# Two banded layers on one core: transposes by halves of rows, and a new order of TensorE's work in a step

## The chip, the cores and the metric

The kernel runs on one core of a Trainium2 chip. The core has a matrix engine (TensorE, PE in the profile, its weight loads shown apart as PEld), a vector engine (DVE), an activation engine (ScalarE, ACT), a general engine (GpSimd, POOL) and a queue that issues nearly all transfers (SyncE, SP). Each engine takes its own instructions in program order and waits on semaphores for the others. TensorE writes to PSUM alone, eight banks of 512 fp32 values on each of 128 partitions; DVE and ScalarE carry the results to SBUF. The metric is the time on the device in microseconds.

## The reference

Two layers of the same form run one after the other on `x` (512 x 512 x 64, fp32): `x = x + layer(_gn(x))`, where `_gn` normalises by groups of two channels over the whole picture. A layer is

```python
xn = _ln(x, norm_scale, norm_bias)                       # over the 64 channels
left = (xn @ Wl + bl) * mask * sigmoid(xn @ Wlg + blg)   # 64 -> 128
right = (xn @ Wr + br) * mask * sigmoid(xn @ Wrg + brg)
out_gate = sigmoid(xn @ Wog + bog)
out = _banded_ingoing(left, right, 4)   # out[i,j,h] = sum over d in -4..4 of left[i+d,i,h] * right[i+d,j,h]
out = _ln(out, out_norm_scale, out_norm_bias) * out_gate
return out @ Wo + bo
```

The kernel does the sum over the band as a matrix product for each channel `h`: a banded 64 x 64 matrix of `left` values times the rows of `right`.

## The kernel before

**Tiling.** Blocks of `S = 64` rows are worked one after the other. A tile has 128 partitions: 64 rows at columns `j` (lower half) and the same 64 rows at columns `256 + j` (upper half). A *unit* is `JU = 8` columns in each half; 16 units (`NU`) make a *chunk* of 128 columns in each half, and there are 18 chunks a layer. The two halves never mix: projections, gates and band products take partitions 0 to 63 and 64 to 127 in separate matmuls, each with its own 64 rows of the matrix engine.

**One step.** The loop in `layer` (L731 on) emits one *step* `t` for every unit. It works on several units at different stages: it loads units ahead, normalises unit `t + 2` (`inner_norm`, POOL), transposes unit `t + 1` so that channels lie on partitions (`transposed`, L430), projects unit `t` to `right` values (`right`, L459, in two halves of four columns), and finishes the output of a unit of 30 steps ago (`outs[t]`). For that it reads the unit's transposed input back from DRAM (`recall`, L590, tile `zg` with two buffers), computes the gates (`gates`, L594), transposes the normalised band sums `on` (`turned`, L613), multiplies them by the gates on DVE into `ZH`, and a step later multiplies by `Wo` (`end`, L643) and adds the residual rows `XR`, which `fetch` (L632) loaded. In layer 1 `sums` adds up statistics for the group norm of layer 2. At the end of a step come zero, one or two `mix` calls (L511), the band products; ten steps of a chunk have 16 of them, six have none. A mix writes its results over `RO`, the buffer of `right` values.

**Order.** All engines get this order as it is written (`keep_in_program_order`, L362, which is why nearly every row of the profile has that line). On TensorE a step is: gates (two matmuls of 64 rows by 128 columns, every fp32 matmul as two instructions), projection (eight matmuls, the same shape), `left` in five early steps, four transposes of `z` and eight of `on` (128 x 128, one instruction each), `end` (16 matmuls of 128 rows by 64 columns), `sums`, and the mixes (64 by 64). ScalarE evacuates gates, sigmoids of the projection, `zT`, then computes the eight `on` of the next step (`norm`, one buffer), then copies mixes. DVE does statistics (`sto` of RO, `sti` of z), the products into RO, ZH, the residual add, and part of the copies. POOL does the affine (`ga`, `gb`), `inner_norm`, the bias onto `XR` (`biased`) and, in every fourth step, the reciprocal root behind `solve`, whose first operation DVE issues (`rs`).

**Queues and buffers.** SyncE issues in a step: loads of z, `zg` for step `t + 2`, `XR` for step `t + 1`, the matrices A (`take_left`), the store of `zT`, the stores of finished rows. An issue that must wait for its buffer holds all behind it. PSUM: pairs of banks (`two_banks`, two of them) for projections and mixes; single banks (`one_bank`, three in layer 1, four in layer 2) for gates, transposes and `end`.

Of the kernel before, what the change touches and what calls it, by code (L numbers as in the profile page):

```python
# [8 lines left out]
F32 = mybir.dt.float32  # L9
I32 = mybir.dt.int32  # L10
AF = mybir.ActivationFunctionType
ALU = mybir.AluOpType
# [4 lines left out]
P = 128  # L17
WIN = 4
NEAR = 2 * WIN + 1
S = 64  # L20
JC = 128
JW = 16
JU = 8
JQ = 4
NU = JC // JU
# [54 lines left out]
def tile_two_banded_layers(  # L80
# [8 lines left out]
    H = layers[0]["Wl"].shape[1]  # L89
    x, out = x[0], out[0]  # L90
# [22 lines left out]
    ident = const.tile([P, P], F32, name="ident")  # L113
# [14 lines left out]
    def one_bank():  # L128
        return ps.tile([P, 512], F32, tag="ps", name="bank")

    def two_banks():
        return ps2.tile([P, 1024], F32, tag="ps2", name="banks")
# [220 lines left out]
    w = views(pack)  # L353
# [66 lines left out]
    def inner_stats(u: Unit, st: bass.AP, k: int):  # L420

        en.vector.bn_stats(st[:, k, :], u.z[:, 2 * k : 2 * k + 2, :].rearrange("p t c -> p c t"))

    def inner_norm(u: Unit):
        z = u.z.rearrange("p (k t) c -> p k t c", t=2)
        m = u.mean.unsqueeze(3).broadcast_to([P, JU // 2, 2, D])
        en.gpsimd.tensor_tensor(z, z, m, ALU.subtract)
        en.gpsimd.tensor_tensor(u.z, u.z, last(u.rs, D), ALU.mult)

    def transposed(u: Unit):  # L430

        u.t = ztp.tile([P, JU // 2, P], F32, tag="zT", name="zT")
        pt = one_bank()
        for k in range(JU // 2):
            en.tensor.transpose(
                pt[:, k * P : (k + 1) * P],
                u.z[:, 2 * k : 2 * k + 2, :].rearrange("p j c -> p (j c)"), ident,
            )
        en.scalar.activation(u.t.rearrange("c k p -> c (k p)"), pt, AF.Identity, bias=1.0)
        if u.near is None:  # L440
            en.sync.dma_start(later[u.at], u.t)

    def place(k: int, e: int) -> int:

        return k // 2 * 4 + 2 * e + k % 2
# [13 lines left out]
    def right(u: Unit, q: int, w: dict):  # L459
        pr = projected(u, q, w["right"]).rearrange("p e k h -> p (e k) h")  # L460
        sg = wk.tile([P, JQ, H], F32, tag="sg", name="sg", bufs=2)
        en.scalar.activation(sg, pr[:, :, H:], AF.Sigmoid)
        en.vector.tensor_tensor(
            RO[:, :, u.c + q : u.c + q + JQ, :],
            pr[:, :, :H].rearrange("p j (h t) -> p h j t", t=2),
            sg.rearrange("p j (h t) -> p h j t", t=2), ALU.mult,
        )
# [31 lines left out]
    def take_left(n: int, h: int) -> bass.AP:  # L499


        A = lp.tile([P, S, HA], F32, tag="A", name="A")
        at = n * size + h * slab + WIN * HA
        for e in range(2):
            en.sync.dma_start(
                A[e * S : (e + 1) * S].rearrange("p i h -> p (i h)"),
                strided(left_of, at, ((S + 2 * WIN) * HA, S), (1, S * HA)),
            )
        return A
# [80 lines left out]
    def recall(o: Out):  # L590
        o.t = ztg.tile([P, JU // 2, P], F32, tag="zg", name="zg")
        en.sync.dma_start(o.t, later[o.at])

    def gates(o: Out, w: dict):  # L594
        b = o.blk
        o.g = []
        pgs = [
            one_bank()[:, : 2 * JQ * b.m].rearrange("h (k p) -> h k p", p=b.m) for e in range(2)
        ]
        for e, pg in enumerate(pgs):  # L600
            part = slice(e * D, (e + 1) * D)
            en.tensor.matmul(
                pg, lhsT=w["gate"][part],
                rhs=o.t[part].rearrange("c k (e p) -> c (k e) p", e=2)[:, :, b.lo : b.hi],
                start=True, stop=True,
            )
        for pg in pgs:
            g = gp.tile([H, 2 * JQ * (S - WIN)], F32, tag="gate", name="gate")
            g = g[:, : 2 * JQ * b.m].rearrange("h (k p) -> h k p", p=b.m)
            en.scalar.activation(g, pg, AF.Sigmoid)  # L610
            o.g.append(g)

    def turned(o: Out, w: dict):  # L613

        b = o.blk
        for e in range(2):
            pt = one_bank()
            for k in range(JQ):
                en.tensor.transpose(
                    pt[:, k * P : (k + 1) * P], o.on[:, place(k, e), :], ident  # L620
                )
            zh = ZH[(2 * o.n + e) % len(ZH)]
            en.vector.scalar_tensor_tensor(
                zh[:, :, : b.m], pt.rearrange("h (k p) -> h k p", p=S)[:, :, b.lo : b.hi], w["ob"], o.g[e],
                ALU.add, ALU.mult,
            )

    def rows_of(v: bass.AP, o: Out, e: int):
# [14 lines left out]
    def end(dst: bass.AP, o: Out, w: dict):  # L643
        m = o.blk.m
        po = one_bank().rearrange("i (j c) -> i j c", c=D)
        for k in range(JQ):
            for e in range(2):
                for n in range(2):

                    en.tensor.matmul(  # L650
                        po[n * S : (n + 1) * S, 2 * k + e, :],
                        lhsT=ZH[(2 * o.n + e) % len(ZH)][:, 2 * k + n, :], rhs=w["Wo"],
                        start=True, stop=True,
                    )
        f = o.xr[: S + m, :, 1 : 1 + 2 * D]
        en.vector.tensor_tensor(
            f, po[: S + m].rearrange("i (k t) c -> i k (t c)", t=2), f, ALU.add
        )
        for e in range(2):
            en.sync.dma_start(rows_of(dst, o, e), o.xr[e * S : e * S + m, :, 1 : 1 + 2 * D])  # L660
# [13 lines left out]
    def layer(src: bass.AP, dst: bass.AP, w: dict, stats: bool, then=None):  # L674
# [32 lines left out]
        def inputs(t: int) -> list:  # L707
            return [d[t] for d in (units, lefts) if t in d]
# [22 lines left out]
        for t in range(min(loads), last_t + 3):  # L731
            if then and t == max(units) + 2:
                then()
            for u in loads.get(t, []):
                if u not in early:
                    load(src, u)
            if t + 2 in outs:
                recall(outs[t + 2])
            if t + 1 in outs:
                fetch(src, outs[t + 1], w, t + 1)  # L740
            for c, h in slabs.get(t, []):
                A[c, h] = take_left(c // per, h)

            for o in looks.get(t, []):
                if sto is None:
# [7 lines left out]
                affine(u, en.vector if u.at < NU + 4 else en.gpsimd)  # L753
            if t % 4 == 3 and t > NU:
                then_affine = affines.pop(t + 1, [])
            if t in outs:
                gates(outs[t], w)

            todo = []
            for at, u in inners.get(t, []):  # L760
# [7 lines left out]
                us.append(u)  # L768
            for v in todo[: len(todo) // 2]:
                inner_stats(*v)  # L770
            if t in units:
                for q in range(0, JU, JQ):
                    right(units[t], q, w)
            if t in lefts:
                for q in range(0, min(JU, NEAR * JQ - lefts[t].near), JQ):
                    left(lefts[t], q, w)
            for u in inputs(t + 2):
                inner_norm(u)
            for u in inputs(t + 1):
                transposed(u)  # L780
            if t in outs:
                turned(outs[t], w)
                biased(outs[t], w, stats)
            for v in todo[len(todo) // 2 :]:
                inner_stats(*v)
# [104 lines left out]
    lp = ctx.enter_context(tc.tile_pool(name="lp", bufs=NA))  # L890
    wk = ctx.enter_context(tc.tile_pool(name="wk", bufs=3))
    onp = ctx.enter_context(tc.tile_pool(name="onp", bufs=1))
    gp = ctx.enter_context(tc.tile_pool(name="gp", bufs=2))

    next(one, None)
    nc.sync.dma_start(pack, spare)
# [35 lines left out]
```

## Time and profile before

| | |
|---|---|
| median of 3 runs | 5074.44 us (5072.06 to 5078.64) |
| profiled execution, its own time | 5074.14 us |
| span from its first to its last instruction | 5072.3 us |
| TensorE busy, matmul / weight load | 4496.1 / 3714.8 us |
| DVE / ScalarE / GpSimd busy | 3732.8 / 3793.8 / 3826.9 us |
| transposes of `on`, 128 x 128 | 4608, mean 274 ns |
| transposes of `z`, 128 x 128 | 2344, mean 290 ns |
| products for the end, `bank<-pack,ZH` | 18432, mean 225 ns |
| granted TensorE clock, mean | 0.978 |

The profile is one execution. Rows name an operation by output and inputs: `bank<-ident,on` is the transpose of `on` into a single bank. Matmuls overlap and their ends are modelled, so a stage's length is read from the start of its first instruction to the start of the next stage's. A bracket in a timeline row is the idle time ahead of it and what ended that. Layer 1 works from about 306 to 2550 us, layer 2 from about 2709 us to the end.

### The profile page before, as it was taken

How to read it: one execution, taken by the hardware profiler on the slowest of the kernel's cores; microseconds unless marked ns; L12 is line 12 of the kernel's file. 1: busy time of each engine (PE TensorE's matmuls, PEld its weight loads, DVE VectorE, ACT ScalarE, POOL GpSimd, SP SyncE). 2: the span in 40 equal slices, each digit the busy share in tenths (PEclk: the TensorE clock that was granted, in tenths of full speed). 3: DMA queues.
4: the chain of work that ended last, by engine and by line, in shares of the span. 5: the costliest groups of instructions: out<-in, count | busy, mean ns of one | idle time of the engine just before them, and what ended most of it. 6: DMA issues, size and time to landing. Idle time of an engine off the chain costs nothing.

```text
span 5072.3 us, 159784 instructions
## 1 busy us (share of the span) xinstructions
PE 4496.1 (89%) x60138; PEld 3714.8 (73%) x60138; DVE 3732.8 (74%) x9445; ACT 3793.8 (75%) x8328; POOL 3826.9 (75%) x4739
## 2 busy tenths in 40 slices
PE   1027999999999999999995599999999999999999
PEld 0015788888888888888873478888888888888886
DVE  6764677777777777777766467777777777777776
ACT  0013788888888888888884268888888888888888
POOL 0037888888888888888733598888888888888863
PEclk9988999999999999999997799999999999999999
DMA  7924666666666666666663456767676776777766
GB/s 317 400 58 125 176 194 197 195 195 193 198 196 195 194 194 197 196 194 198 189 171 102 106 176 201 202 198 202 200 205 201 202 203 200 202 204 204 204 182 173
DMA packets 905291, 981.45 MB, mean 193 GB/s; under 512 B 114210, under 2 KB 641608, under 8 KB 900168
## 3 DMA queue, kind: packets, MB, share of 16 engines
q1 hardware_dynamic: 897248, 948.49, 63.5%
q10 hardware_dynamic: 7272, 22.73, 1.1%
q8 instruction: 477, 7.82, 0.7%
q14 instruction: 294, 2.41, 0.2%
HBM read 658.42 MB, written 312.46 MB: 191 GB/s over the span
## 4 chain that ended last, share of the span: by engine, by line
PE 72%; POOL 9%; DMA 6%; DVE 4%; ACT 3%; issue 2%; SPq 2%; another core or an unknown queue 0%; ACTq 0%; POOLq 0%; DVEq 0%
PE banks L362 38%; PE bank L362 32%; POOL z L362 6%; ACT on L362 2%; DMA left_of<-nothing 2%; PE acc L362 2%; SPq L362 2%; DVE RO L362 1%; POOL XR L362 1%; DMA gn_x<-in_x_dram 1%; POOL rsqrt L362 1%; DVE ZH L362 1%; DMA XR<-mid_x 1%; DVE sto L362 1%; ACT gate L362 1%
## 5 line engine op out<-in xcount | busy, mean ns | idle before, releaser
L362 ACT ACTIVATE on<-RO,nm,rs 128x128 f32<-128x128 f32 x4608 | 1879.2, 495 | 172.4 <-PE bank L362 169.9
L362 PE MATMUL banks<-pack,zT 64*128 64x256 f32 x9360 | 1213.1, 389 | 137.0 <-ACT zT L362 76.6
L362 PEld LDWEIGHTS banks<-pack,zT 64*128 64x128 f32 x9360 | 967.2, 192 | 419.8 <-issue 180.4
L362 PE MATMUL banks<-RO,A 64*64 64x128 f32 x18432 | 1154.5, 277 | 15.6 <-DVE RO L362 15.4
L362 PEld LDWEIGHTS banks<-RO,A 64*64 64x64 f32 x18432 | 1082.4, 183 | 43.6 <-DVE RO L362 18.6
L362 DVE TENSOR_TENSOR RO<-banks,sg 128x512 f32<-128x512 f32 x1152 | 747.0, 681 | 258.8 <-ACT sg L362 258.0
L362 ACT ACTIVATE sg<-banks 128x512 f32<-128x512 f32 (+1 forms) x1188 | 682.7, 589 | 319.8 <-PE banks L362 208.0
L362 DVE COPY RO<-banks 128x512 f32<-128x512 f32 x360 | 248.9, 692 | 869.1 <-ACT RO L362 869.1
L362 DVE BATCH_NORM_STATS2 sto<-RO 128x6 f32<-128x256 f32 x2304 | 797.5, 411 | 1.2
L362 DVE SCALAR_TENSOR_TENSOR ZH<-bank,pack,gate 128x448 f32<-128x448 f32 (+1 forms) x1152 | 740.0, 682 | 37.6 <-ACT gate L362 36.3
L362 POOL TENSOR_TENSOR z<-z,gb 128x512 f32<-128x512 f32 x536 | 687.7, 1283 | 42.1
L362 POOL TENSOR_TENSOR z<-z,ga 128x512 f32<-128x512 f32 x536 | 687.5, 1283 | 0.1
L362 PE MATMUL bank<-zg,pack 64*128 64x448 f32 (+1 forms) x2304 | 657.4, 595 | 18.9 <-DVE ZH L362 15.8
L362 PE MATMUL bank<-pack,ZH 128*64 128x64 f32 x18432 | 663.5, 225 | 2.8 <-ACT zT L362 0.3
L362 ACT ACTIVATE gate<-bank 128x448 f32<-128x448 f32 (+1 forms) x1152 | 567.1, 542 | 126.6 <-PE bank L362 125.8
L362 PEld LDWEIGHTS bank<-pack,ZH 128*64 128x64 f32 x18432 | 584.0, 138 | 100.3 <-ACT zT L362 83.2
L362 POOL TENSOR_TENSOR z<-z,rs 128x512 f32<-128x512 f32 x586 | 618.0, 1055 | 45.9
L362 PE MATMUL bank<-ident,on 128*128 128x128 f32 x4608 | 616.6, 274 | 14.7 <-ACT gate L362 12.1
L362 POOL TENSOR_TENSOR z<-z,sti 128x512 f32<-128x512 f32 x586 | 623.8, 1065 | 0.0
L362 ACT COPY RO<-banks 128x512 f32<-128x512 f32 x792 | 441.2, 586 | 239.0 <-PE banks L362 237.8
L362 PEld LDWEIGHTS bank<-ident,on 128*128 128x128 f32 x4608 | 519.7, 141 | 74.0 <-ACT on L362 24.3
L362 POOL TENSOR_TENSOR XR<-XR,pack 120x512 f32<-120x512 f32 (+1 forms) x352 | 418.4, 1189 | 192.4 <-DMA XR<-mid_x 90.4
(137 smaller groups left out, 3927.6 us busy)
## 6 DMA issues: line engine op xcount, KB each, us to landing
later<-zT SPq DMA_DIRECT2D x576, 256.0 KB
A<-left_of SPq DMA_DIRECT2D x576, 256.0 KB
zg<-later SPq DMA_DIRECT2D x576, 256.0 KB
z<-in_x_dram SPq DMA_DIRECT2D x576, 128.0 KB
z<-mid_x SPq DMA_DIRECT2D x576, 128.0 KB
gn_x<-in_x_dram SPq DMA_DIRECT2D x16, 4096.0 KB
XR<-in_x_dram SPq DMA_DIRECT2D x448, 112.0 KB
mid_x<-XR SPq DMA_DIRECT2D x448, 112.0 KB
```

The costliest lines, as they stand in the source:

```text
L362: return lambda *a, **k: tc.keep_in_program_order(f(*a, **k))
```

## The change

It has four parts. (1) Every transpose of a 128-partition tile becomes two, one for partitions 0 to 63 and one for 64 to 127, each into a bank of its own, in turn. They have the shape of the projection's matmuls, 64 rows by 128 columns, with 64 moving columns. `turned` therefore fills its two banks by halves of rows, where they were by channel groups, and `ZH`, the gate tile and the reads in `end` are laid out to match. The gates of both halves share one tile of one buffer. `transposed` takes a pair of banks (`two_banks`) for most units, so that one activation still carries the result out. (2) That activation and the store move into `kept`. (3) In a step TensorE's order becomes: first half of the projection, gates, second half, `left`, `turned`, `transposed`, then `end` and the rest as before. (4) `recall` goes behind `fetch` and `take_left` in SyncE's queue.

```diff
     def transposed(u: Unit):
+        if u.near is None and u.at > NU:
+            u.pt = [two_banks().rearrange("c (n x) -> c n x", n=2)[:, :, : JU // 2 * S]]
+            halves = [u.pt[0][:, n] for n in range(2)]
+        else:
+            halves = [one_bank()[:, : JU // 2 * S] for n in range(2)]
+            u.pt = [h.unsqueeze(1) for h in halves]
+        for k in range(JU // 2):
+            for n in range(2):
+                part = slice(n * S, (n + 1) * S)
+                en.tensor.transpose(
+                    halves[n][:, k * S : (k + 1) * S],
+                    u.z[part, 2 * k : 2 * k + 2, :].rearrange("p j c -> p (j c)"),
+                    ident[part, part],
+                )
+
+    def kept(u: Unit):
         u.t = ztp.tile([P, JU // 2, P], F32, tag="zT", name="zT")
-        pt = one_bank()
-        for k in range(JU // 2):
-            en.tensor.transpose(
-                pt[:, k * P : (k + 1) * P],
-                u.z[:, 2 * k : 2 * k + 2, :].rearrange("p j c -> p (j c)"), ident,
-            )
-        en.scalar.activation(u.t.rearrange("c k p -> c (k p)"), pt, AF.Identity, bias=1.0)
+        to = u.t.rearrange("c k (n p) -> c n k p", n=2)
+        for n, pt in enumerate(u.pt):
+            en.scalar.activation(
+                to[:, n : n + pt.shape[1]], pt.rearrange("c n (k p) -> c n k p", p=S),
+                AF.Identity, bias=1.0,
+            )
         if u.near is None:
             en.sync.dma_start(later[u.at], u.t)
...
-        for pg in pgs:
-            g = gp.tile([H, 2 * JQ * (S - WIN)], F32, tag="gate", name="gate")
-            g = g[:, : 2 * JQ * b.m].rearrange("h (k p) -> h k p", p=b.m)
-            en.scalar.activation(g, pg, AF.Sigmoid)
-            o.g.append(g)
+        g = gp.tile([H, 4 * JQ * (S - WIN)], F32, tag="gate", name="gate")
+        for e, pg in enumerate(pgs):
+            en.scalar.activation(
+                g[:, e * n : (e + 1) * n].rearrange("h (k p) -> h k p", p=b.m), pg, AF.Sigmoid
+            )
+        o.g = g[:, : 2 * n].rearrange("h (x n p) -> h n x p", n=2, p=b.m)
 
     def turned(o: Out, w: dict):
         b = o.blk
+        pts = [one_bank().rearrange("h (x p) -> h x p", p=S) for n in range(2)]
         for e in range(2):
-            pt = one_bank()
             for k in range(JQ):
-                en.tensor.transpose(
-                    pt[:, k * P : (k + 1) * P], o.on[:, place(k, e), :], ident
-                )
-            zh = ZH[(2 * o.n + e) % len(ZH)]
+                for n, pt in enumerate(pts):
+                    part = slice(n * S, (n + 1) * S)
+                    en.tensor.transpose(
+                        pt[:, e * JQ + k, :], o.on[part, place(k, e), :], ident[part, part]
+                    )
+        for n, pt in enumerate(pts):
             en.vector.scalar_tensor_tensor(
-                zh[:, :, : b.m], pt.rearrange("h (k p) -> h k p", p=S)[:, :, b.lo : b.hi], w["ob"], o.g[e],
-                ALU.add, ALU.mult,
+                ZH[(2 * o.n + n) % len(ZH)][:, :, : b.m], pt[:, :, b.lo : b.hi], w["ob"],
+                o.g[:, n], ALU.add, ALU.mult,
             )
...
-                        lhsT=ZH[(2 * o.n + e) % len(ZH)][:, 2 * k + n, :], rhs=w["Wo"],
+                        lhsT=ZH[(2 * o.n + n) % len(ZH)][:, e * JQ + k, :], rhs=w["Wo"],
...
-            if t + 2 in outs:
-                recall(outs[t + 2])
             if t + 1 in outs:
                 fetch(src, outs[t + 1], w, t + 1)
             for c, h in slabs.get(t, []):
                 A[c, h] = take_left(c // per, h)
+            if t + 2 in outs:
+                recall(outs[t + 2])
...
-            if t in outs:
-                gates(outs[t], w)
...
             if t in units:
-                for q in range(0, JU, JQ):
-                    right(units[t], q, w)
+                right(units[t], 0, w)
+            if t in outs:
+                gates(outs[t], w)
+            if t in units:
+                right(units[t], JQ, w)
             if t in lefts:
                 for q in range(0, min(JU, NEAR * JQ - lefts[t].near), JQ):
                     left(lefts[t], q, w)
             for u in inputs(t + 2):
                 inner_norm(u)
+            if t in outs:
+                turned(outs[t], w)
             for u in inputs(t + 1):
                 transposed(u)
+                kept(u)
             if t in outs:
-                turned(outs[t], w)
                 biased(outs[t], w, stats)
...
-    gp = ctx.enter_context(tc.tile_pool(name="gp", bufs=2))
+    gp = ctx.enter_context(tc.tile_pool(name="gp", bufs=1))
```

## The prediction

> **What bounds the kernel now.** I read the page first, then the timeline of TensorE over single steps, then the timelines of the other engines where TensorE waits, then the waits over six chunks of each layer. A chunk is 16 steps; mixes are spread over them as 2, 1, 2, 2, 1, 2, 1, 2, 2, 1 and six steps without any. From the page:
>
> ```profile
> PE 4496.1 (89%) x60138; PEld 3714.8 (73%) x60138; DVE 3732.8 (74%) x9445; ACT 3793.8 (75%) x8328; POOL 3826.9 (75%) x4739
> ...
> PE 72%; POOL 9%; DMA 6%; DVE 4%; ACT 3%; issue 2%; SPq 2%; another core or an unknown queue 0%; ACTq 0%; POOLq 0%; DVEq 0%
> ```
>
> TensorE carries 72% of the chain, but four engines are near each other. One step of layer 2 with one mix, TensorE's timeline:
>
> ```profile
> 3511.56 1.02 PE L362 MATMUL bank<-zg,pack 64*128 64x448 f32 x4
> 3512.42 1.89 PE L362 MATMUL banks<-pack,zT 64*128 64x256 f32 x16
> 3514.24 0.66 PE L362 MATMUL bank<-ident,z 128*128 128x128 f32 x4
> 3514.74 1.04 PE L362 MATMUL bank<-ident,on 128*128 128x128 f32 x8
> 3515.71 1.15 PE L362 MATMUL bank<-pack,ZH 128*64 128x64 f32 x32
> 3516.79 2.10 PE L362 MATMUL banks<-RO,A 64*64 64x128 f32 x32
> 3518.82 1.02 PE L362 MATMUL bank<-zg,pack 64*128 64x448 f32 x4
> ```
>
> From start to start: gates 0.86, projection 1.82, transposes of z 0.50, of `on` 0.97, end 1.08, mix 2.03, in all 7.26 without a stall. Two mixes make 9.09, none 5.22; layer 1 adds 0.47 for the sums (9.56 with two mixes). So the ten steps with mixes are TensorE's. The six without are not; layer 2, TensorE and POOL:
>
> ```profile
> 3461.35 0.66 PE L362 MATMUL bank<-ident,z 128*128 128x128 f32 x4 [0.95 <-POOL z L362]
> ...
> 3467.25 0.66 PE L362 MATMUL bank<-ident,z 128*128 128x128 f32 x4 [0.60 <-POOL z L362]
> ...
> 3473.13 0.66 PE L362 MATMUL bank<-ident,z 128*128 128x128 f32 x4 [0.59 <-POOL z L362]
> ...
> 3482.24 2.00 PE L362 MATMUL banks<-RO,A 64*64 64x128 f32 x30 [1.28 <-DVE RO L362]
> ```
>
> ```profile
> 3446.46 1.18 POOL L362 TENSOR_TENSOR XR<-XR,pack 120x512 f32<-120x512 f32 x1 [2.60 <-DMA XR<-mid_x]
> ...
> 3454.59 0.29 POOL L362 TENSOR_TENSOR rsqrt<-rs 128x64 f32<-128x64 f32 x1 [4.36 <-DVE rs L362]
> ```
>
> The stretch begins at 3439.46 and ends at 3475.67. DVE works from 3441.03 without a gap (two steps with eight statistics of RO each), its `rs` releases POOL's reciprocal root at 3454.59, POOL takes 4.5 us for that and 2.1 for z, and then 5.89 a step (the transposes wait at 3461.35, 3467.25, 3473.13). That is 33.7 us in which TensorE decides nothing. POOL's floor: in the six chunks from 3118.87 to 3843.32 it waits 49.8 us of 724.45, so it needs 112.4 us a chunk, against 120.7 taken; in layer 1 (1058.46 to 1808.89) 75.9 of 750.43, again 112.4, against 125.1 (8.3 and 12.7 of slack).
>
> **What the Trainium skill says.** "TensorEngine Tiling (Array Packing)", Key Properties: tiles work in parallel, and a change of tiling mode drains the array. The trace agrees: eight pairs of projection instructions fill 1.73 us, one pair in 0.216, so the stage's 1.82 has 0.09 of drain; the z stage has 0.06 over four transposes of 0.110 (a first weight load in the open). The same page, Restrictions: column tiling excludes transposes of fp32; row tiling, which this change uses, isn't named. "TensorE: Matmul & The Clock Gate", LDWEIGHTS: a load costs by its columns, not its rows, so a half as long as a whole; the trace agrees, ordinary loads of 128 columns last 185 to 192 ns with 64 rows, of 64 columns 138 with 128 rows. "PSUM — Partial Sum Buffer", PSUM bank collisions: different row tiles must not be in one bank at once; the change gives each half its own. For half transposes no run here shows these last points yet.
>
> **The change, part by part.** *Transposes.* Twelve of 128 moving columns a step become 24 of 64. Old price: eight starts in 1.04 less the last one's 0.273 over seven, 0.110 each. New price, not in the trace: nearest is `end`, 64 moving columns, pairs of tiles side by side, (1.15 - 0.222) / 15 = 0.06 a pair. The load of 128 columns must hide behind the pair before it: a transpose's load lasts 141 ns in the page's terms, `end`'s 64 ordinary columns 138, an ordinary load of 128 columns 185 to 192. I take it that a half keeps the 141 form, so 0.06 a pair holds. Bounds: 0.055 a pair if only columns count; 0.11 if the load is of the ordinary, longer form; 0.22 if the two tiles don't overlap at all. At 0.06, twelve pairs are 0.72 us.
> *Order.* Projection, gates, `turned` and `transposed` now share one tiling; one change of mode (0.09 + 0.06) goes. Projection and both transposing stages: 1.82 + 0.50 + 0.97 = 3.29 before; 1.73 + 0.72 + 0.09 (the drain before `end`) = 2.54 after. **0.75 us a step.**
> *ScalarE.* Same number of activations, in the order sigmoid, gates, sigmoid, zT, `on`; cost 0. Its wait of about 0.34 a step for TensorE ahead of `on` goes, since `turned` is over before zT. It is no bound: from a gate at 3477.90 to `on` at 3480.18 it needs 2.28, and 3.13 for eight `on`; 16 x 5.41 and 22 copies of 0.53 are 98 a chunk. `kept` issues the store of zT as before.
> *Gate tile, one buffer for both halves.* The next gates wait for both ZH operations. In a mixing step ZH ends near 3508.4 and the next gate runs at 3512.6; where DVE is late, ZH ends at 3446.5 and the gate starts at 3446.9, and a sigmoid of 0.5 now comes between. Cost 0, if that cover went some 0.1.
> *PSUM.* `transposed` takes a pair of banks, so a first mix now needs the pair of the second half of the projection, not of the first: one DVE multiply (681 ns) later. In most mixing steps DVE has finished it 4.2 to 4.6 us after the step's start (its next operation starts at 3515.80 and 3507.11 in the steps from 3511.56 and 3502.47) and TensorE comes to the mix at 4.47: 0 to 0.2. In the first mixing step of a chunk DVE is late already (3482.24, the 1.28 above): there the 0.75 is not gained, and about 0.6 is lost. In layer 1 TensorE comes 0.47 later; I take 0.4 lost of the 0.75.
> *SyncE's queue.* `zg` for two steps on waits for this step's gates (two buffers). Until now `XR` (two issues, 0.86) and A (1.09) stood behind it; now they go first, and behind the waiting `zg` stand the stores of zT and `XR` and the next z loads. The gates move by 0.95 in the step; `zg` has two steps, 10 us and more, so 0. POOL's waits for `XR` (13.0 and 7.8 in six chunks) go, but straight into its wait for `rs` (4.36 right behind the 2.60), which DVE sets: 0; 1 to 2 us a chunk if DVE were not late.
> *Sum.* Stretch without mixes: the 33.7 stays; after the last z TensorE did 2.54 (z, `on`, end), now 0.24 + 0.09 + 1.08 = 1.41, since `turned` is done during the wait: -1.1. Mixing steps: nine by 0.75 is -6.75; the first one +0.6 in layer 2, -0.35 in layer 1. Layer 2: -7.3, 113.4 a chunk, only 1.0 above POOL's floor. Layer 1: -8.2, 116.9. Both kinds of work run together for 288 - 30 = 258 steps a layer, 16.1 chunks: 15.5 x 16.1 = -250. In the 30 steps that only finish, layer 1 is TensorE's (138.7 busy of 139.0): 0.64 a step, -20; layer 2's tail is ScalarE's (136.7 of 152), 0. The first 30 steps of a layer have slack: 0. In all -270: span 5072.3 to 4802. The profiled execution took 5074.14, 1.84 more than its span, and the median is 5074.44: about **4805 us**.
>
> **The rivals.** *The gain leaks into coupled waits* (layer 2 without slack on POOL; first mixes waiting each step for DVE). Speaks for it: 1.0 us a chunk of slack. Against: POOL is a step and a half ahead of need in most steps. Half the gain: 4935. *The transposes get no cheaper* (0.11 a pair by the longer load): only the 0.15 of the mode change, nine steps, 1.4, and 0.3 at the last z, less the 0.6: -1.1 a chunk, 36 us: 5035. For: no half transpose is in the trace. Against: projection and gates, the same tile, overlap fully. *Slower:* the two row tiles of a transpose exclude each other and each half keeps its 0.11, so a pair takes 0.22: twelve pairs 2.64 for 1.32, less 0.15, +1.17 a step. TensorE's own chunk (6 x 5.22 + 4 x 7.26 + 6 x 9.09 = 114.9; with 16 x 0.47 for the sums 122.4) grows by 18.7, to 133.6 and 141.1: +12.9 and +16, by 16.1: +465, 5540. It decides from 0.1225 a pair (twelve are 1.47). Against it: pairs of all other matmuls start 7 ns apart.
>
> **How the numbers follow.** As worked 64% (4740, POOL's floor in both layers, 21.0 x 16.1 = 338 saved, to 4880); leaking 12% (to 4985); no cheaper 12% (to 5064); no difference 2%; slower 10%. Faster 0.88, same 0.02, slower 0.10; 0.2% is some 10 us, about what these runs can tell. Leaving out the top of the third case and the slower one, the range is 4740 to 5020.
>
> **What would show it.** TensorE's row for `on` at x9216, 64 rows, some 24 half transposes of a step in 0.75 us; steps of 8.3 and 6.5 us with mixes; POOL's waits for `XR` near 0; POOL busy near 80% and up. Wrong: pairs over 0.06, or TensorE idle ahead of `banks<-RO,A` in every step on DVE, or POOL z ahead of the transposes in mixing steps.

## The result, and the profile after

The changed kernel takes 5229.43 us (median of 4 runs, 5225.33 to 5244.22) against 5074.06 us before: 1.031 times the time, 95% interval 1.0289 to 1.0332. The forecast was 4805 us, faster; the measured time is 424 us above it, outside the range, and on the other side of no change.

From the page of the changed kernel, the busy times of the engines:

```profile
PE 4235.4 (81%) x67090; PEld 3585.8 (69%) x67090; DVE 3698.6 (71%) x9445; ACT 3742.6 (72%) x8372; POOL 3821.9 (73%) x4739
```

TensorE did get less to do: 4235.4 us busy for 4496.1. It was 89% busy and is 81% busy, so some 412 us of idle time have come in its place (988 us idle in a span of 5223.5, against 576 in 5072.3). The chain of work that ended last breaks off in this profile after some 3% of the span, so the place has to be found from waits and timelines.

The forecast's picture of a step does exist. TensorE's timeline of the changed kernel, layer 2, one step with one mix (to be held against the step from 3511.56 before):

```profile
3531.76 1.13 PE L362 MATMUL banks<-pack,zT 64*128 64x256 f32 x8
3532.73 0.92 PE L362 MATMUL bank<-zg,pack 64*128 64x448 f32 x4
3533.48 1.03 PE L362 MATMUL banks<-pack,zT 64*128 64x256 f32 x8
3534.35 0.67 PE L362 MATMUL bank<-ident,on 64*128 64x64 f32 x16
3534.84 0.42 PE L362 MATMUL banks<-ident,z 64*128 64x64 f32 x8
3535.19 1.15 PE L362 MATMUL bank<-pack,ZH 128*64 128x64 f32 x32
3536.27 2.10 PE L362 MATMUL banks<-RO,A 64*64 64x128 f32 x32
3538.31 1.13 PE L362 MATMUL banks<-pack,zT 64*128 64x256 f32 x8
```

From start to start it is 6.55 us, where the forecast had 6.5, and the 24 halves take 0.84 with the change of mode behind them (0.49 and 0.35). Sixteen halves of `on` start within 0.44 us in such steps, 0.062 from pair to pair of row tiles; the forecast's price was 0.06. But only two of the ten mixing steps of a chunk look like this, 8 and 9, in both layers. They are also the only two, of all sixteen, in which DVE has no statistics of RO to do. The other mixing steps look like the one from 3586.10. Its timeline, TensorE and DVE:

```profile
3586.10 1.13 PE L362 MATMUL banks<-pack,zT 64*128 64x256 f32 x8
...
3586.83 0.69 DVE L362 COPY RO<-banks 128x512 f32<-128x512 f32 x1 [3.74 <-ACT RO L362]
...
3587.44 1.40 DVE L362 BATCH_NORM_STATS2 sto<-RO 128x6 f32<-128x256 f32 x4
...
3588.68 0.66 PE L362 MATMUL bank<-ident,on 64*128 64x64 f32 x16
3588.75 0.48 DVE L362 BATCH_NORM_STATS2 sti<-z 128x6 f32<-128x128 f32 x2
...
3589.16 1.26 DVE L362 TENSOR_TENSOR RO<-banks,sg 128x512 f32<-128x512 f32 x2
...
3589.97 0.46 PE L362 MATMUL banks<-ident,z 64*128 64x64 f32 x8 [0.63 <-DVE RO L362]
```

Read it from the bottom. The transposes of z write into `banks`, a pair, and there are two pairs: one holds the second half of the projection, so they need the one with the first half (the wait below ends with the multiply that frees it). DVE empties that one by its first multiply (`RO<-banks,sg`, at 3589.16), which has three things ahead of it on its engine: the copy of the last mix (which waits for the mix to end), 1.3 us of statistics of RO and 0.4 of z. TensorE is at the transposes of z 3.08 us after the start of the step (2.58 to the start of `on`, 0.49 for its halves), and they start at 3.87: a wait of 0.79 for a saving of 0.75. The step takes 7.38 (before 7.26).

TensorE's waits over the whole execution, us in total, times, longest; before:

```profile
PE banks L362 <- DVE RO L362: 67.9, 54, 10.7
```

and after:

```profile
PE banks L362 <- DVE RO L362: 375.6, 342, 10.4
```

That is 308 us more of one wait, and it is the wait of the z transposes: by shapes, their group reads

```profile
L362 PE MATMUL banks<-ident,z 64*128 64x64 f32 x4336 | 252.5, 232 | 394.7 <-DVE RO L362 333.3 <-POOL z L362 31.5 <-issue 10.4
```

The first mixing step of a chunk, number 0, is worse. Layer 1, TensorE and DVE:

```profile
1331.67 1.31 DVE L362 SCALAR_TENSOR_TENSOR var<-sto,pack 128x32 f32<-128x32 f32 x1
...
1333.02 1.30 DVE L362 TENSOR_SCALAR var<-var 128x32 f32<-128x32 f32 x1
...
1334.46 1.40 DVE L362 BATCH_NORM_STATS2 sto<-RO 128x6 f32<-128x256 f32 x4
...
1335.78 1.27 DVE L362 TENSOR_TENSOR RO<-banks,sg 128x512 f32<-128x512 f32 x2
...
1336.60 0.46 PE L362 MATMUL banks<-ident,z 64*128 64x64 f32 x8 [2.84 <-DVE RO L362]
...
1336.99 1.93 PE L362 MATMUL bank<-pack,ZH 128*64 128x64 f32 x32
```

The five operations of `solve` (1331.03 to 1334.56) and the statistics stand ahead of the multiply. TensorE idles 2.84 us, and then its `end` takes 1.93 instead of 1.15; the trace has the granted clock at 0.5 from 1337.08 to 1340.50.

Where the time went, us a chunk, from the starts on TensorE (means of 12 or 13 chunks a layer). "Joint" is used from here on for the part of a layer in which both kinds of work run; the 30 steps ahead of it are its head, the 30 behind it its tail. The forecast's change stands beside the measured one:

| | before | after | change | forecast |
|---|---|---|---|---|
| layer 1, step 0 | 9.8 | 12.7 | +2.9 | -0.35 |
| layer 1, nine other mixing steps | 78.7 | 79.1 | +0.4 | -6.75 |
| layer 1, six without mixes | 36.6 | 36.8 | +0.2 | -1.1 |
| layer 2, step 0 | 10.1 | 12.5 | +2.4 | +0.6 |
| layer 2, nine other mixing steps | 74.5 | 76.2 | +1.7 | -6.75 |
| layer 2, six without mixes | 36.2 | 36.6 | +0.4 | -1.1 |

That is 23.5 us a pair of chunks (one of each layer) above the forecast, and by the 16.1 chunks of a joint part some 378 us. The heads of the layers are 9.8 and 12.2 longer (forecast 0), the tail of layer 1 is 5.1 longer (forecast -20). Together that is about the 424 us that were missed.

### The profile page after: what moved, and what is told of

Same layout as the page of the kernel before. It is cut to its first block, busy times and chain, and to the rows that moved or that the text cites. A ratio compares the mean times of both kernels' runs of the same rounds, so it can differ in the third digit from the quotient of the medians.

```text
span 5223.5 us, 173594 instructions
## 1 busy us (share of the span) xinstructions
PE 4235.4 (81%) x67090; PEld 3585.8 (69%) x67090; DVE 3698.6 (71%) x9445; ACT 3742.6 (72%) x8372; POOL 3821.9 (73%) x4739
## 5 line engine op out<-in xcount | busy, mean ns | idle before, releaser
L362 PE MATMUL banks<-pack,zT 64*128 64x256 f32 x9360 | 1334.0, 407 | 114.0 <-ACT zT L362 57.8
L362 PEld LDWEIGHTS banks<-pack,zT 64*128 64x128 f32 x9360 | 891.1, 195 | 479.3 <-DVE RO L362 186.8
L362 PE MATMUL banks<-RO,A 64*64 64x128 f32 x18432 | 1170.5, 279 | 14.3 <-ACT zT L362 14.3
L362 PEld LDWEIGHTS banks<-RO,A 64*64 64x64 f32 x18432 | 1098.5, 184 | 41.2 <-ACT zT L362 17.0
L362 PE MATMUL bank<-pack,ZH 128*64 128x64 f32 x18432 | 693.7, 231 | 5.5 <-ACT gate L362 5.1
L362 PEld LDWEIGHTS bank<-pack,ZH 128*64 128x64 f32 x18432 | 611.7, 143 | 47.4 <-ACT gate L362 9.2
L362 ACT ACTIVATE zT<-banks 128x512 f32<-128x512 f32 x542 | 323.9, 598 | 438.0 <-PE banks L362 397.3
L362 PE MATMUL banks<-ident,z 64*128 64x64 f32 x4336 | 252.5, 232 | 394.7 <-DVE RO L362 333.3
L362 DVE BATCH_NORM_STATS2 sti<-z 128x6 f32<-128x128 f32 x2344 | 548.4, 282 | 14.2 <-POOL z L362 14.2
L362 PE MATMUL bank<-zg,pack 64*128 64x448 f32 (+1 forms) x2304 | 554.8, 552 | 4.0 <-DVE ZH L362 2.4
```

What stands on the lines that cost most here:

```text
L362: return lambda *a, **k: tc.keep_in_program_order(f(*a, **k))
```

## The experiments

All ratios are to the kernel before, run on the same chip. Differences in us between two versions are of their medians; some versions ran on different chips, on which the kernel before had medians of 5069 to 5074 us. The question that the trace leaves: is it the pair of banks that z now takes, the statistics ahead of the multiply on DVE, the granted clock, or one of the other parts of the change?

### Statistics of RO behind the gates

In the changed kernel, the block of `out_stats` is issued between the two halves of the projection instead of ahead of both, so DVE multiplies the first half first.

```diff
-            for o in looks.get(t, []):
-                ...
             if t in units:
                 right(units[t], 0, w)
             if t in outs:
                 gates(outs[t], w)
+            for o in looks.get(t, []):
+                ...
             if t in units:
                 right(units[t], JQ, w)
```

> The changed kernel, with DVE's statistics of RO (four or eight operations, 1.3 or 2.6 us) moved behind the gates, so that DVE multiplies the first half of the projection ahead of them. Theory A: the loss comes from the pair of PSUM banks that the z transposes now take; it is free only when DVE has multiplied the first half of the projection, and that stands behind the copy of the last mix and the statistics (TensorE waits until 3.87 us in a mixing step, where it could go on at 3.08). Then the wait goes here: steps of about 6.5 and 8.4 us in layer 2, 7.0 and 8.9 in layer 1, 4800 to 4880 us in all. Theory B: the loss comes from the new order (gates behind half a projection, ScalarE's sigmoids and the single banks): then little changes, above 5150 us. Theory C: the multiply is late anyway, as its sigmoid is: 5000 to 5150 us.

Measured 4935.04 us, ratio 0.9731 (0.9715 to 0.9747): 294 us below the changed kernel by the order of one block on DVE. It lies outside each of the bands that were set, between the first and the third: the statistics ahead of the multiply are the larger part of the loss against the forecast, and not all of it. A mixing step of layer 2 in it, DVE and TensorE:

```profile
3668.97 0.69 DVE L362 TENSOR_TENSOR RO<-banks,sg 128x512 f32<-128x512 f32 x1
...
3669.58 1.39 DVE L362 BATCH_NORM_STATS2 sto<-RO 128x6 f32<-128x256 f32 x4
3669.74 0.66 PE L362 MATMUL bank<-ident,on 64*128 64x64 f32 x16
3670.24 0.41 PE L362 MATMUL banks<-ident,z 64*128 64x64 f32 x8
```

The multiply is over at 3669.66, the transposes of z follow those of `on` without a gap, and the step is 6.53 (from 3667.16). The nine mixing steps are 72.5 in layer 1 and 70.1 in layer 2, where the forecast had 72.0 and 67.8. Step 0 is still 11.2 and 11.7.

### The z transposes whole, in a single bank

The changed kernel, with z transposed as before (four 128 x 128, a single bank, taken ahead of the two of `turned`).

```diff
-        if u.near is None and u.at > NU:
-            u.pt = [two_banks()...]
-        ...
+            en.tensor.transpose(
+                u.pt[:, k * P : (k + 1) * P],
+                u.z[:, 2 * k : 2 * k + 2, :].rearrange("p j c -> p (j c)"), ident,
+            )
...
+            for u in inputs(t + 1):
+                u.pt = one_bank()
             if t in outs:
                 turned(outs[t], w)
```

> The changed kernel, with only the transposes of z as they were before: whole, 128 x 128, into one single bank that is taken ahead of those of the transposes of on. Order, queue, gate tile and the halves of on stay changed. Theory A (the pair of banks): no wait for DVE is left ahead of the z transposes; the halves of on save 0.40 us a step and the change of tiling is as before, so about 4900 to 4960 us. Theory B (the order): above 5150 us.

Measured 5239.78 us, 1.0337 (1.0322 to 1.0353): no gain in all. But the layers part. Layer 2, with four single banks, falls from 2011.4 to 1898.7 us in the steps with both kinds of work. Layer 1, with three, rises from 2067.1 to 2217.1. (Before, the two joint parts were 1940.0 and 2010.2.) So layer 2 points to the pair, and in layer 1 what replaces it is worse: from 1060 to 1800 us TensorE waits 104.5 us there for DVE's multiplies into ZH, and 3.8 before.

### The same, with the bank taken later and ZH written behind the transposes

```diff
+        u.pt = one_bank()
         for k in range(JU // 2):
...
             for u in inputs(t + 1):
                 transposed(u)
                 kept(u)
             if t in outs:
+                gated(outs[t], w)
                 biased(outs[t], w, stats)
```

(`gated` is the loop with the two ZH multiplies, taken out of `turned`.)

> The run with z whole again (a single bank for z, halves of on, the new order and queue), with one more change: the multiplies into ZH are written behind z's activation, so that the next single bank to come free is z's and not one that DVE still has to read. In the run with z whole layer 2 was faster than before (1899 against 1940 us while both kinds of work run), layer 1 slower (2217 against 2010), where the end waited for DVE's ZH at 4.82 us in a step. Theory A, widened to single banks: layer 1 falls to about 1950, layer 2 stays near 1900, 4950 to 5000 us. If the order is at fault in layer 1: layer 1 stays above 2150, 5200 us.

Measured 5242.05 us, 1.0336 (1.032 to 1.0351), the same; layer 1 takes 2219.5. Layer 1, TensorE and DVE:

```profile
1405.41 1.15 PE L362 MATMUL bank<-pack,ZH 128*64 128x64 f32 x32 [1.11 <-DVE ZH L362]
```

```profile
1403.49 1.27 DVE L362 TENSOR_TENSOR RO<-banks,sg 128x512 f32<-128x512 f32 x2
1404.68 1.27 DVE L362 SCALAR_TENSOR_TENSOR ZH<-bank,pack,gate 128x448 f32<-128x448 f32 x2
```

The stall has the same form one stage later: `end` starts when DVE's first ZH multiply is over, and that stands behind the same late multiplies. Why `end` is tied to DVE here with either way of taking the bank isn't settled. Nor was `turned` ahead of `transposed`, which both versions keep, run by itself.

### The z halves in two single banks, layer 2 alone

```diff
-        if u.near is None and u.at > NU:
+        if pairs and u.near is None and u.at > NU:
...
-                transposed(u)
+                transposed(u, stats)
                 kept(u)
             if t in outs:
+                gated(outs[t], w)
```

(`stats` is true in layer 1, which keeps the pair.)

> The changed kernel, but in layer 2, which has four single banks, the halves of z go to two single banks instead of a pair (two activations of 256 carry them out), and the multiplies into ZH are written behind them. DVE's order is untouched. Theory A: layer 2 loses its wait for the first multiply and comes to the steps that the prediction had, 6.5 and 8.4 us, about 1825 us (1800 to 1870) while both kinds of work run, against 2011 in the changed kernel; layer 1 stays at 2067; 5020 to 5070 us in all. If something else holds layer 2: its part above 1950, 5150 us or more.

Measured 5101.98 us, 1.0062 (1.0047 to 1.0077). Layer 2 falls to 1905.8, less far than expected; layer 1 stays at 2072.0. In layer 2 the wait for DVE has gone, and `end` now waits for ScalarE's evacuation of z (TensorE):

```profile
3561.62 1.15 PE L362 MATMUL bank<-pack,ZH 128*64 128x64 f32 x32 [0.47 <-ACT zT L362]
```

With the statistics behind the gates as well:

> The run before this one (layer 2's z halves in single banks), and in both layers the statistics of RO behind the gates, as in the run that moved them alone (layer 1 1914, layer 2 1880 us there). Theory A: layer 1 as there, layer 2 1820 to 1865, in all 4860 to 4910 us, the fastest so far. If the two remedies overlap wholly: 4930.

Measured 4947.1 us, 0.9754 (0.974 to 0.9769), no better than moving the statistics alone: layer 1 gains what it gained there (1914.8 against 1913.7), and layer 2 stays where the single banks had put it (1902.5; with the statistics alone 1879.9). The two remedies act on the same wait.

### The pair alone, in the kernel before

The other way round: nothing of the change but the place where z goes.

```diff
-        pt = one_bank()
+        pair = u.near is None and u.at > NU
+        pt = two_banks()[:, : JU // 2 * P] if pair else one_bank()
```

> The kernel before with one change: the whole transposes of z go to the first bank of a pair of banks instead of a single bank. No half transposes, old order. Theory A (the pair is free only after DVE's multiply of the first half): in a mixing step z's transposes go from 2.68 to about 3.87 us after the step's start, with the eight of on, the end and the mixes behind them; about 1.2 us a mixing step, ten steps a chunk, 32 chunks: 5350 to 5480 us. If the pair costs nothing by itself: 5060 to 5090 us.

Measured 5707.97 us, 1.1263 (1.1246 to 1.128): some 640 us more than before, more than I expected. TensorE, two steps without mixes of layer 1:

```profile
1398.77 0.63 PE L362 MATMUL banks<-ident,z 128*128 128x128 f32 x4 [1.39 <-DVE RO L362]
...
1405.79 0.63 PE L362 MATMUL banks<-ident,z 128*128 128x128 f32 x4 [1.30 <-DVE RO L362]
```

I had counted on mixing steps. Those without mixes go from 36.6 to 43.6 us a chunk in layer 1 as well: the first multiply, the transposes of z, their evacuation, ScalarE's eight `on` and its next gates and sigmoid follow each other without slack, and one turn of this loop takes 7.02 us (1398.77 to 1405.79). The pair for z is by itself enough for a loss larger than that of the whole change.

### The remaining parts, one by one, in the kernel before

`recall` behind `fetch` and `take_left`:

> The kernel before, with only the queue changed: the recall of zg behind the loads of XR and A. Theories A and B both: POOL's waits for XR go, into its wait for rs, which DVE sets; 5060 to 5080 us. If the later zg matters: over 5090 us.

Measured 5068.38 us, 0.9995 (0.9987 to 1.0004): nothing, as the forecast had it and for its reason: POOL's waits for `XR` fall from 187.8 to 118.5 us in all, and its wait for `rs` rises from 358.8 to 432.1.

Half of the projection, gates, the other half:

```diff
-                for q in range(0, JU, JQ):
-                    right(units[t], q, w)
+                right(units[t], 0, w)
+            if t in outs:
+                gates(outs[t], w)
+            if t in units:
+                right(units[t], JQ, w)
```

> The kernel before with one change: TensorE does half the projection, then the gates, then the other half. Theory A (PSUM buffers tie TensorE to DVE, through the z transposes' pair): the order itself costs nothing, 5055 to 5090 us. Theory B (the order makes ScalarE, and so all behind it, late): most of the loss is here, above 5150 us.

Measured 5065.71 us, 0.9991 (0.9984 to 0.9998): less than 0.2%.

`turned` by halves of rows, with its gate tile and ZH, in the old order:

> The kernel before in its old order, with only the transposes of on by halves (and the gate tile and ZH laid out to match). Theory A: eight transposes of 0.110 us become eight pairs of 0.058, 0.41 us less, and one change of tiling is added, 0.15; 0.26 us in each mixing step and less elsewhere, 4970 to 5010 us. Theory B says the same here, since the order is the old one. If half transposes cost more than pairs of 0.06: about 5074 or more.

Measured 5014.46 us, 0.9891 (0.9877 to 0.9906). The halves of `on` are worth some 55 us by themselves. They leave a change of mode between the whole transposes of z and the halves of `on`, 0.59 from start to start for 0.49; a step with one mix in layer 2 is 7.0 for 7.3 all the same.

### TensorE kept busy through the stall

In many steps 0 and 10 of the changed kernel the granted clock is at half for 3.4 us behind the stall. Here `turned` repeats its sixteen transposes five times in those two steps, writing the same values; in the joint parts the repeats lie mostly inside the wait.

```diff
-        for e in range(2):
+        for e in times * list(range(2)):
...
-                turned(outs[t], w)
+                turned(outs[t], w, 5 if t % NU in (0, 10) else 1)
```

> The changed kernel, with the 16 half transposes of on done five times over in the first step with mixes and the first without (the two steps of a chunk in which TensorE stalls for some 2.3 to 3.7 us ahead of z's transposes and in or behind which the trace shows a window of 3.4 us at half the clock). The repeats take about 1.9 us and lie in the stall; they write the same values again. Theory (a long stall costs a second time, by the clock): most of the 50 windows of half clock go, each worth 1.4 to 1.7 us, 5140 to 5180 us. If the low clock hides behind DVE and ScalarE: 5215 to 5240 us. If the repeats don't fit the stall: slower.

Measured 5199.09 us, 1.0263 (1.0246 to 1.028). The shortfall of the clock (one less the granted share, times how long it lasted) falls from 42.6 and 49.1 us in the two layers' joint parts to 1.7 and 6.8. Of these 83 us, 30 come back. In the joint parts of the profiled execution it is 36; in the tails, where there is little stall to lie in, the repeats cost some 15. The clock is a small part of the loss.

In the version with the statistics behind the gates, the same repeats:

> The fastest so far, the changed kernel with the statistics of RO behind the gates (4935 us), with the same repeats. It has 4 such windows in layer 1 and 13 in layer 2. By the clock: 15 windows of 1.5 us less, 4905 to 4925 us; if the repeats no longer find a stall to lie in, up to 60 us slower, 4990 us.

Measured 5005.36 us, 0.9877 (0.9862 to 0.9892), 70 us slower than without them: step 10, which no longer stalls there, grows from 5.9 to 7.0 us in layer 1, and the tail by 9.

### What is left: step 0

At 4935 us step 0 was the largest single piece (11.2 and 11.7 us, where TensorE needs 8.9 and 8.4, as in step 8). DVE in that step has `solve` ahead of the multiply. So `solve` of a chunk's last step was moved behind the next step's first half of the projection:

```diff
                 right(units[t], 0, w)
+            for args in pending:
+                solve(w, *args)
+            pending = []
...
-                    solve(w, us, os, st, so)
+                    if t % NU == NU - 1:
+                        pending.append((us, os, st, so))
+                    else:
+                        solve(w, us, os, st, so)
```

> The version with RO's statistics behind the gates, and `solve` of every fourth step's last unit of a chunk also moved, from the end of that step to behind the first half of the next step's projection, so that in step 0 of a chunk its small operations no longer stand on DVE ahead of the first multiply. If those operations were the larger part of what that version still loses in step 0 (about 3 to 6 us in each of some 32 chunks): 4840 to 4900. If the wait only passes on, to the second half's multiply or to GpSimd, whose own floor is 112 us a chunk: 4925 to 4945, the same as without it. If `solve` now comes too late for GpSimd, whose affine waits for it: above 4950.

Measured 4964.04 us, 0.9781 (0.9756 to 0.9805): 29 us slower than without it. The steps with both kinds of work take 1911.8 us in layer 1 (1913.7 without) and 1912.9 in layer 2 (1879.9 without). Layer 2, TensorE in step 0, and the stretch of the mix with its clock (the columns are PE, PEld, DVE, ACT and POOL busy with instructions, clock, DMA share, GB/s):

```profile
3635.25 0.46 PE L362 MATMUL banks<-ident,z 64*128 64x64 f32 x8 [0.72 <-DVE RO L362]
...
3638.87 6.56 PE L362 MATMUL banks<-RO,A 64*64 64x128 f32 x64 [2.08 <-DVE RO L362]
```

```profile
3638.87:3645.30 6.43, 6.43 (x64) 6.36 (x64) 1.73 (x3) 1.63 (x4) 5.78 (x12) 0.55 0.64 190
```

The transposes of z now come 3.97 us after the step's start, and 6.24 in the step from 3614.91 of the version without the edit. But `solve` and the statistics stand ahead of the second multiply instead, so the mix waits, and in layer 2 it then runs at about half the clock: 14.1 us for the step. In layer 1 the mix waits too (about 1.5 us), its clock stays full, and the step is 11.1, as before the edit. The number lies in the last band of the expectation, but not for the reason given there: what the middle band describes happened, the wait passed on, and the half clock under the mix, 2.6 us in each step 0 of layer 2, came on top. It is one profile of a version whose runs spread from 4951 to 4973 us.

Both multiplies first, then `solve`, then the statistics:

```diff
             if t in units:
                 right(units[t], JQ, w)
+            for args in pending:
+                solve(w, *args)
+            pending = []
+            for o in looks.get(t, []):
+                ...
```

> Both halves of the projection, with both of DVE's multiplies, ahead of RO's statistics and of the delayed `solve`, so that neither the transposes of z nor the first mix of step 0 stands behind them. If what is left of the loss is DVE's order in step 0 (in the run before this one TensorE is idle there for 2.1 us on the second multiply, its mix then runs at half the clock, 6.3 for 3.7 us): step 0 falls from 14.1 in layer 2 and 11.1 in layer 1 to 8.4 to 9.5, and the time to 4840 to 4890. If ScalarE, 7.8 us busy in that step, or GpSimd's floor takes over: 4890 to 4940. If RO's statistics now come too late for ScalarE's `norm` or for the next mix: above 4950.

Measured 4993.03 us, 0.9845 (0.9829 to 0.9862). Step 0 falls to 9.6 and 9.4 us, near what was expected of it, and the time does not fall; it lies in the last band. The nine mixing steps go from 72.5 and 70.1 to 73.1 and 72.7, those without from 35.4 and 35.6 to 37.3 and 36.6. One such mixing step, number 4 of a chunk of layer 2, DVE and TensorE:

```profile
3572.58 1.30 DVE L362 TENSOR_SCALAR var<-var 128x32 f32<-128x32 f32 x1
...
3574.02 0.69 DVE L362 COPY RO<-banks 128x512 f32<-128x512 f32 x1
...
3574.76 1.46 PE L362 MATMUL banks<-pack,zT 64*128 64x256 f32 x6 [2.31 <-DVE RO L362]
```

Here `solve` of step 3 or 7 holds up the copy of the last mix, and with it the pair that the second half of the projection needs; the step is 10.65. No order of DVE that was tried wins back what separates 4935 from the forecast: each frees one buffer earlier and another one later.

## Why the prediction was wrong

**The failed step.** It is the paragraph on PSUM. It said rightly that `transposed` takes a pair of banks, and then asked only what that does to the mix behind it: "one DVE multiply (681 ns) later", "0 to 0.2". It did not ask what the transposes of z themselves wait for. With two pairs, their own pair is the one of the projection's first half, and its release is DVE's first multiply. The forecast checked DVE's second multiply against TensorE's 4.47 us in the step. The first multiply, with the statistics ahead, starts to matter at 3.08. From the profile of before its time could be read; DVE in the step from 3511.56:

```profile
3512.30 0.69 DVE L362 COPY RO<-banks 128x512 f32<-128x512 f32 x1 [0.93 <-ACT RO L362]
...
3512.91 1.39 DVE L362 BATCH_NORM_STATS2 sto<-RO 128x6 f32<-128x256 f32 x4
...
3514.22 0.48 DVE L362 BATCH_NORM_STATS2 sti<-z 128x6 f32<-128x128 f32 x2
...
3514.62 1.27 DVE L362 TENSOR_TENSOR RO<-banks,sg 128x512 f32<-128x512 f32 x2
```

The copy waits for the mix, and the first of the two multiplies (0.68 us) ends at 3515.29, 3.73 us into the step: 0.65 later than TensorE comes to the transposes of z in the new order, which is most of the 0.75. Before, they came at 2.68 and waited for no pair. In the step of the changed kernel shown above the multiply ends at about 3.75. Moving the statistics gives 294 us back; the pair alone costs 640.

**Why the whole saving went.** The wait closes a loop: mix, ScalarE's and DVE's copies, statistics, multiply, transposes of z, `end`, next mix. Inside it TensorE's own work is only a part, and halving a transpose shortens nothing that the loop waits for; so nine mixing steps came out at +0.4 and +1.7 us instead of -6.75. The loop is read from DVE's and TensorE's order; what shows it is that steps 8 and 9, without the statistics, take the forecast's 8.4 and 6.5 us in layer 2, and the other seven come near them once the statistics are moved.

**Step 0.** The forecast saw DVE late there and took +0.6 and -0.35; it was +2.4 and +2.9. The term took the wait at the mix as before and added one multiply; in fact `solve` and the statistics now hold up z, `end` and the mix in a row.

**Head and tail.** The head was put at 0 for its slack, and lost 10 to 12 us a layer. The heads are back at 232.0 and 232.7 us (before 232.5 and 232.3) when z is transposed whole into a single bank, and layer 2's is 233.3 with the halves in two single banks; with the pair alone in the kernel before they are 245.1 and 241.8. So this too comes with the pair. For the tail of layer 1 the forecast was -20, since TensorE was busy in it for 138.7 of 139.0 us. That figure is of the stretch from 2411 to 2550 us, which lies in the joint part. (The text on the profile before lets layer 1 end at about 2550 us; its tail runs on from 2552 to about 2709.) In the tail itself TensorE is busy for 142.9 of 156.1, so the term had no ground. A step of the tail after the change, TensorE:

```profile
2680.55 0.22 PE L362 MATMUL bank<-ident,on 64*128 64x64 f32 x1
2681.42 0.71 PE L362 MATMUL bank<-ident,on 64*128 64x64 f32 x15 [0.65 <-ACT gate L362]
```

Halves in turn need both banks from the second transpose on, where the old order needed the second one four transposes later; one of three single banks still holds the gates. From gates to `end` it is 2.41 us now, and 2.32 in the step from 2623.05 before. Some 3 of the 5.1 us come from two steps alone, 9.25 for 7.73; why these two is open.

**What held.** The price of a half (0.06 a pair forecast, 0.062 measured), and with it the weight load: 139 ns for a half, 141 for a whole. (That loads cost by their columns alone isn't so plain in the trace as the forecast had it: the mixes' loads of 64 columns and 64 rows last 183 ns, nearly as long as the ordinary ones of 128.) These held too: steps of 6.5 and 8.4 us in layer 2 where nothing hinders them, the order of the projection and the queue at 0, GpSimd not the bound. The rival that ended slower was a price of 0.22 a pair; the loss came, by another mechanism. The first rival, "first mixes waiting each step for DVE", was nearest, with the wrong instruction waiting, and half the gain left where none was. The second of the signs of being wrong, TensorE idle on DVE in every step, is close to what the trace shows: eight of ten mixing steps, though ahead of `banks<-ident,z` and not of `banks<-RO,A`.

**Evacuation.** The Trainium skill, "TensorEngine Tiling (Array Packing)", PSUM Bottleneck, says in general what the forecast left out: "Tiling speeds up TensorE but not PSUM evacuation". The trace agrees: TensorE's busy time fell by 261 us and its wait for DVE's evacuation rose by 308. Which bank the faster stage waits for, and what stands ahead of the engine that frees it, had to be read from the trace.

**What stays open.** The version with the statistics moved, 4935 us, is the fastest of all that ran, 2.7% below the kernel before, and 130 us above the forecast. Some 93 of them lie in the joint parts (nearly all in the nine mixing steps, 2.9 us a pair of chunks, and in step 0, 2.8), the rest in heads and tail. The orders tried on DVE moved that loss and didn't remove it; no single cause is shown. The loss of layer 1 with z whole is open too. Halves of `on`, queue and the order of the projection cost nothing there when run alone, so `turned` ahead of `transposed` with three single banks is the suspect. With z in the pair and the statistics moved it doesn't stop layer 1 from falling to 1913.7.

## What to carry to other kernels

When an edit gives an instruction another buffer, ask first what that instruction now waits for: which one releases the buffer, what stands ahead of the releaser on its engine, and when it ends in the step; only then what the next user loses. A faster stage is worth its time only if it is not put behind the slowest evacuation of a loop; the same edit with the releasing instruction moved ahead of work that is needed only later went from +3.1% to -2.7%. Test a suspected buffer alone in the old kernel: here one changed place showed a loss larger than that of the whole change.

## What the runs showed of the hardware

**The clock can fall after short stalls.** The Trainium skill, "TensorE: Matmul & The Clock Gate", What's actually happening, describes a state of half the clock that comes after at least one idle window of about 3.4 us. The trace agrees on the half and on the 3.4 us: windows of that length at 0.5 (one of 6.8), 24 of them in layer 1's joint part and 29 in layer 2's, where before had one each. It differs on what brings them, since most stalls ahead of them are shorter. Of 54 stalls of TensorE of 1.75 us and more in these parts (the longest is 4.0), 46 have one in them or within 3.5 us behind; five windows of layer 1 have only stalls of 1.2 to 1.5 near them. Length alone doesn't settle it: of 99 such stalls in the kernel with the pair alone, 16 brought one. What it costs differs. Taking the windows away was worth 30 us of 83, so the time lost there is mostly time in which TensorE would have waited. With `solve` moved, windows of 6.8 us fell on the mix of nearly every step 0 of layer 2, and 64 products took 6.49 us for 3.87, with nothing to hide it. The mean clock of a run doesn't tell this: the changed kernel's was 0.933 to 0.96 in runs of much the same time, and in its trace 140 of the 352 us of shortfall lie ahead of layer 1, where TensorE has little to do.

**Small DVE operations can last as long as GpSimd's beside them.** The operations of `solve` mostly take either 0.14 to 0.2 us or 0.7 to 1.3. In the version with the statistics moved, two of the long ones run from 3617.61 to 3618.92 and from 3619.05 to 3620.30, and GpSimd's `ga` and `gb` multiplies from 3617.61 to 3618.88 and from 3618.95 to 3620.25. The Trainium skill, "SBUF — State Buffer", SBUF: two separate sides, tells of a pair of ports that the two engines hold in turn for a whole instruction. These two fit that, though one operation of 0.18 us began with `gb`, at 3618.96; no run here tests it. The forecast had put no price on `solve`.
